# Attention: holding the packed reciprocal and the division's product behind later additions in VectorE's queue

## The chip, the cores and the metric

The program runs on one core of a Trainium2 chip. The metric is the device time of one execution in microseconds (us). Before the change it is 2966.07 us, the median of three runs (2962.72 to 2966.71). The profiled execution of the same kernel spans 2957.4 us; the times inside the stage below are read from it.

## The reference

The whole program is a convolution-attention block, a multi-head attention and a mixture of experts, one after the other. Only the attention is touched: 4096 tokens, 256 channels, 8 heads of 32 channels each.

```python
q, k, v = jnp.split(x @ w_qkv + b_qkv, 3, axis=-1)        # then split into heads
dots = jnp.einsum('bhid,bhjd->bhij', q, k) * d ** (-0.5)
attn = jax.nn.softmax(dots, axis=-1)
out = jnp.einsum('bhij,bhjd->bhid', attn, v)
...
return out @ w_out + b_out
```

The softmax is computed as exp(dots), summed over the keys, and the product with v is divided by that sum afterwards.

## The kernel before

**Loops.** The attention (L958 to L1057) runs over 8 chunks of 512 queries (`qc`), and in each over two groups of four heads (`g`). That makes 16 groups, which are numbered 0 to 15 here in the order in which they run, so that an even number has g = 0 and an odd one g = 1. Each group runs over 32 tiles of 128 keys (`i` from 0 to 31).

**One tile of keys.** TensorE multiplies keys with queries for the four heads (L968) into two PSUM tiles of two banks each (`ps_two`, three of which exist, so a tile takes two out of three). ScalarE takes the exponential of each pair of heads (L978) into one SBUF tile `pe` of 128 x 2048 numbers; four such tiles exist (`bufs=4`), so tile i needs the buffer of tile i - 4. A `pe` has two readers: TensorE multiplies it with the values, one tile later, into `acc` (L938, called by `use`), and VectorE adds it to `total`, the running sum over the keys, in two additions of 128 x 1024 (L985). Tile 0 is not added by itself: the first addition is of tiles 0 and 1. Tile 31 isn't added either, but goes straight to the denominator by a multiplication with ones. So a group has 60 additions. `total` is a single buffer.

**The end of a group.** It is spread over the first tiles of the next group. `behind` hands a list of stages to `tick`, and every tile calls `tick` once, after its additions are written. At tile 0 `take` does the last product and copies `acc` to `attnT` (ScalarE, L1003). At tile 1 `pack` multiplies `total` with ones on TensorE (the denominators, L1006), copies them to SBUF (ScalarE, L1024), and sends one row of each head to DRAM and back in another layout, as 128 x 16 numbers (`dens`, `some`, L1026 and L1027, from the SP queue). Since the first addition of a group overwrites `total`, it waits for the multiplication of tile 1. Some tiles later `turn` takes the reciprocal of the 128 x 16 numbers on VectorE (L1032), stores it to DRAM (L1033) and reads it back, spread over each head's 32 partitions (L1036, four transfers). Later still `spread` multiplies the 128 x 512 numbers of `attnT` by it on VectorE (L1009). The last group divides at once, without this round trip.

**Projections.** In every group with g = 1 except that of the first chunk (groups 3, 5, ... 15), four tiles (i = 3, 10, 17, 24) also project the previous chunk: two products on TensorE (L919), an addition and two statistics instructions on VectorE (L922, L740, L741).

**What sets the order on an engine.** The text of the program isn't the order of an engine's queue: the framework's scheduler orders the instructions of each engine, subject to the dependencies that it knows. In the text, `turn` stands behind the additions of tile 6, and `spread` behind those of tile 11. In the queue of VectorE the scheduler has both earlier:

```
L985 total<-pe        x2     tile 1
L985 total<-total,pe  x2     tile 2
L1032 reciprocal             `turn`
L985 total<-total,pe  x3     tile 3, and half of tile 4
L1009 act<-act,rec           `spread`
L985 total<-total,pe  x53    the rest
```

Of the kernel before, what the change touches and what calls it, by code (L numbers as in the profile page):

```python
# [111 lines left out]
def tile_conv_attn_hybrid(ctx: ExitStack, tc: tile.TileContext, a: dict, out: bass.AP):  # L112
    nc = tc.nc
# [4 lines left out]
    def psum(name, bufs):  # L118
        return tc.tile_pool(name=name, bufs=bufs, space=PSUM)
# [20 lines left out]
    def tok(i):  # L140
        return slice(P * i, P * (i + 1))

    def chunk(i):
        return slice(CH * i, CH * (i + 1))
# [18 lines left out]
    def behind(*stages):  # L163

        chains.append(list(stages))

    def tick():
        due = chains[:]
        chains.clear()
        for stages in due[::-1]:  # L170
            stages[0]()
        chains.extend(stages[1:] for stages in due if stages[1:])

    def flush():
        while chains:
            tick()
# [584 lines left out]
    with ExitStack() as phase:  # L761
# [163 lines left out]
        with tc.If(tame > 0) as branch:  # L925
            with (
                tc.tile_pool(name="a_work", bufs=1) as work,
                tc.tile_pool(name="a_dram", bufs=1, space=bass.MemoryType.DRAM) as dram,
                psum("a_ps1", 1) as ps,
            ):  # L930

                def two_banks():
                    return ps.tile([P, 2, CH], F32, tag="two", name="ps_two", bufs=3)

                def per_head(to, lhsT, rhs, start, stop):

                    for hd in range(4):
                        nc.tensor.matmul(  # L938
                            to[D * hd : D * (hd + 1), :],
                            lhsT(hd),  # L940
                            rhs[:, hd, :],
                            start=start,
                            stop=stop,
                            skip_group_check=True,
                        )

                dens = dram.tile([4, CH], F32, name="dens")  # L950
                recs = dram.tile([4, CH], F32, name="recs")
                packed = lambda z: z.rearrange("h (j c) -> (h j) c", c=CH // D)
                done = []

                def den_bank():
                    return ps.tile([P, CH], F32, tag="den", name="ps_den")

                for qc in range(NCH):  # L958
                    for g in range(KC):
                        acc = ps.tile([P, CH], F32, tag="acc", name="ps_acc")  # L960
                        den = []
                        total = work.tile([P, 4, CH], F32, name="total")
                        first = None
                        for i in range(NT):
                            sc = [two_banks() for _ in range(2)]
                            for hd in range(4):
                                hs = slice(D * hd, D * (hd + 1))
                                nc.tensor.matmul(  # L968
                                    sc[hd // 2][:, hd % 2, :],
                                    qk[hs, 1, g, tok(i)],  # L970
                                    qk[hs, 0, g, chunk(qc)],
                                    start=True,
                                    stop=True,
                                )
                            pe = work.tile([P, 4, CH], F32, name="pe", bufs=4)
                            pairs = [slice(0, 2), slice(2, 4)]
                            for pair, s in zip(pairs, sc):
                                nc.scalar.activation(pe[:, pair, :], s, AF.Exp, scale=C**-0.5)  # L978
                            if i == 0:
                                first = pe  # L980
                            elif i < NT - 1:

                                for pair in pairs:
                                    to = total[:, pair, :]
                                    nc.vector.tensor_add(  # L985
                                        to, first[:, pair, :] if i == 1 else to, pe[:, pair, :]
                                    )
                            tick()

                            def use(i=i, pe=pe, acc=acc, den=den, g=g):  # L990
                                values = lambda hd: v[:, i, P * g + D * hd : P * g + D * (hd + 1)]
                                per_head(acc, values, pe, i == 0, i == NT - 1)
                                if i == NT - 1:
                                    den.append(den_bank())
                                    per_head(den[0], lambda hd: ones, pe, True, False)

                            stages = [use]
                            if i == NT - 1:
                                to = attnT[:, g, chunk(qc)]

                                def take(use=use, to=to, acc=acc):
                                    use()
                                    nc.scalar.copy(to, acc)  # L1003

                                def whole(den=den, total=total):
                                    per_head(den[0], lambda hd: ones, total, False, True)  # L1006

                                def times(rec, to=to):
                                    nc.vector.tensor_mul(to, to, rec)  # L1009

                                def divide(den=den, whole=whole, times=times):
                                    whole()
                                    rec = work.tile([P, CH], F32, tag="rec", name="rec")
                                    nc.vector.reciprocal(rec, den[0])
                                    times(rec)

                                held = []

                                def pack(den=den, whole=whole, held=held):
                                    whole()
                                    rec = work.tile([P, CH], F32, tag="rec", name="rec")
                                    nc.scalar.copy(rec, den[0])  # L1024
                                    some = work.tile([P, CH // D], F32, name="some")
                                    nc.sync.dma_start(dens, rec[::D, :])  # L1026
                                    nc.sync.dma_start(some, packed(dens))  # L1027
                                    held.append(some)

                                def turn(held=held):  # L1030
                                    some = held.pop()
                                    nc.vector.reciprocal(some, some)  # L1032
                                    nc.sync.dma_start(packed(recs), some)  # L1033
                                    rec = work.tile([P, CH], F32, tag="rec", name="rec")
                                    for hd in range(4):
                                        nc.sync.dma_start(  # L1036
                                            rec[D * hd : D * (hd + 1), :], recs[hd].partition_broadcast(D)
                                        )
                                    held.append(rec)

                                def spread(times=times, held=held):
                                    times(held.pop())

                                wait = [lambda: None] * 4
                                if qc == NCH - 1 and g == KC - 1:
                                    stages = [take, divide]
                                else:
                                    stages = [take, pack, *wait, turn, *wait, spread]
                            behind(*stages)


                            if qc and g == KC - 1 and i in (3, 10, 17, 24):
                                done.append(NB * (qc - 1) + len(done) % NB)
                                project(den_bank(), done[-1])
                flush()
                for i in range(len(done), NT):
                    project(two_banks()[:, 0, :], i)  # L1057
# [55 lines left out]
    with ExitStack() as phase:  # L1113
# [49 lines left out]
        with ExitStack() as routing:  # L1163
# [126 lines left out]
            for n in range(2):  # L1290
# [13 lines left out]
                for i8 in range(0, NT, G):  # L1304
                    some = lambda v, n: v[:, i8 : i8 + G].unsqueeze(1).to_broadcast([P, n, G])
# [169 lines left out]
```

## Time and profile before

| what | value |
|---|---|
| time, median of 3 runs | 2966.07 us |
| span of the profile | 2957.4 us |
| TensorE, matmul, busy over the whole span | 2817.9 us (95%) |
| VectorE busy | 2080.4 us (70%) |
| ScalarE busy | 1526.6 us (52%) |
| first exponential to last group's division | about 1157 to 2342 us |
| reciprocal of the round trip, L1032 | 15, of 246 ns each |
| product of the division, L1009 | 16, of 692 ns each |

The attention takes about 40% of the span. The profile gives for every engine its busy time, and for every instruction the idle time of its engine just before it and what ended that idle time (the releaser). The timeline lists instructions in order of time, with runs of equal ones merged; "x53" is 53 instructions in one stretch. TensorE's ends are modelled by the profiler, so its busy time says less than that of the others.

### The profile page before, as it was taken

The numbers are of one execution on the slowest core, as the hardware profiler recorded it, in microseconds if no ns is written. First come the engines' busy times: TensorE is split into PE (matmuls) and PEld (weight loads), VectorE is DVE, ScalarE is ACT, GpSimd is POOL, SyncE is SP. The second block draws the span as 40 slices with busy tenths as digits, with TensorE's granted clock in tenths as the row PEclk, the third lists the DMA queues.
The fourth block names the chain that finished last, engine by engine and source line by source line (L and its number), as shares of the span: only waits on it lengthen the run. The fifth ranks groups of instructions, "written<-read, shape, count | busy, mean of one in ns | idle before, by whom it ended". The sixth has DMA issues, their size and how long they took to land.

```text
span 2957.4 us, 63169 instructions
## 1 busy us (share of the span) xinstructions
PE 2817.9 (95%) x26422; PEld 1366.7 (46%) x26422; DVE 2080.4 (70%) x2975; ACT 1526.6 (52%) x2110; POOL 741.5 (25%) x832
## 2 busy tenths in 40 slices
PE   7899999989999989999999999999999789999996
PEld 5456442736644354222222222222222268888884
DVE  5776767577586877999999999999999821111113
ACT  2242323124233214888888888888888632222222
POOL 4085858109485621000000000000000022222220
PEclk9999999999999989999999999999999879999997
DMA  2000000000000000000000000000000155565565
GB/s 86 6 2 4 2 3 2 7 1 3 4 2 3 1 19 1 5 5 5 5 5 5 5 5 5 5 5 5 5 5 5 35 187 195 191 201 188 189 200 198
DMA packets 92634, 133.29 MB, mean 45 GB/s; under 512 B 16914, under 2 KB 73976, under 8 KB 92340
## 3 DMA queue, kind: packets, MB, share of 16 engines
q1 hardware_dynamic: 78008, 101.12, 10.4%
q0 software_dynamic: 6912, 18.88, 2.2%
q10 hardware_dynamic: 7420, 9.15, 0.9%
q8 instruction: 211, 3.46, 0.5%
q14 instruction: 83, 0.68, 0.1%
HBM read 111.00 MB, written 18.12 MB: 44 GB/s over the span
## 4 chain that ended last, share of the span: by engine, by line
PE 56%; issue 1%; DVE 1%; DMA 1%; ACT 1%; POOL 0%; ACTq 0%; POOLq 0%; DVEq 0%
PE ps_two L968 19%; PE ps_acc L938 16%; PE ps_yp L1396 8%; PE ps_hp L1389 8%; PE ps_den L938 1%; PE ps_den L919 1%; DMA y<-yrows 1%; PE ps_acc L1313 1%; ACT z L1197 1%; PE ps_tp L1364 1%; DVE total L985 1%; DVE t L1433 0%; DMA xs<-zrows,source 0%; ACT pe L978 0%; PE ps_two L919 0%
## 5 line engine op out<-in xcount | busy, mean ns | idle before, releaser
L978 ACT ACTIVATE pe<-ps_two 128x1024 f32<-128x1024 f32 x1024 | 993.1, 1022 | 157.6 <-PE ps_two L968 151.2
L985 DVE TENSOR_TENSOR total<-total,pe 128x1024 f32<-128x1024 f32 x928 | 1057.9, 1213 | 0.0
L968 PE MATMUL ps_two<-qk 32*128 32x512 f32 x4096 | 636.3, 640 | 3.6 <-POOLq L925 1.9
L938 PE MATMUL ps_acc<-pe,v 128*32 128x512 f32 x4096 | 546.4, 605 | 0.1
L533 ACT COPY sm<-ps_sc 128x384 f32<-128x384 f32 (+4 forms) x486 | 232.4, 512 | 463.0 <-PE ps_sc L657 269.4
L537 POOL TENSOR_TENSOR sm<-sm,mask 128x192 f32<-128x192 f32 (+3 forms) x460 | 379.8, 861 | 228.1 <-ACT sm L533 227.6
L968 PEld LDWEIGHTS ps_two<-qk 32*128 32x128 f32 x4096 | 211.9, 183 | 418.7 <-PE ps_two L968 221.3
L537 DVE TENSOR_TENSOR sm<-ps_sc,mask 128x384 f32<-128x384 f32 (+3 forms) x708 | 323.5, 516 | 92.4 <-PE ps_sc L657 91.2
L1390 ACT ACTIVATE hid<-ps_hp,cols 128x256 f32<-128x256 f32 x288 | 136.3, 473 | 382.5 <-PE ps_hp L1389 382.5
L1239 POOL MEMSET on<- 128x256 f32 x1 | 0.3, 311 | 1190.4 <-PE ps_den L938 1190.4
L938 PEld LDWEIGHTS ps_acc<-pe,v 128*32 128x32 f32 x4096 | 80.9, 108 | 389.2 <-issue 376.0
L1389 PE MATMUL ps_hp<-xe,w 128*128 128x256 f32 x1152 | 256.9, 381 | 0.0
L1396 PE MATMUL ps_yp<-w,hid 128*128 128x256 f32 x1152 | 254.6, 379 | 0.0
L657 PE MATMUL ps_sc<-qk 32*128 32x192 f32 (+3 forms) x2688 | 243.8, 444 | 4.6 <-DVE sm L537 2.9
L1396 PEld LDWEIGHTS ps_yp<-w,hid 128*128 128x128 f32 x1152 | 216.5, 190 | 28.0
L1389 PEld LDWEIGHTS ps_hp<-xe,w 128*128 128x128 f32 x1152 | 208.6, 190 | 41.9 <-ACT hid L1390 5.0
L673 PE MATMUL ps_acc<-sm,v 128*32 128x192 f32 (+3 forms) x2688 | 216.6, 423 | 0.8 <-POOL sm L537 0.8
L1368 DVE TENSOR_SCALAR xe<-ps_tp,cols 128x256 f32<-128x256 f32 x72 | 35.8, 539 | 248.7 <-PE ps_tp L1364 228.7
L537 POOL TENSOR_TENSOR sm<-sm,ycut 128x384 f32<-128x384 f32 (+4 forms) x150 | 150.7, 1024 | 145.3 <-ACT sm L533 145.1
L657 PEld LDWEIGHTS ps_sc<-qk 32*128 32x128 f32 x2688 | 125.5, 185 | 123.0 <-DVE sm L537 70.1
L537 DVE TENSOR_TENSOR sm<-ps_sc,ycut 128x512 f32<-128x512 f32 (+4 forms) x250 | 127.5, 561 | 71.2 <-PE ps_sc L588 69.2
L1398 DVE TENSOR_TENSOR y<-ps_yp,b 128x256 f32<-128x256 f32 x72 | 30.5, 424 | 208.0 <-PE ps_yp L1396 208.0
(235 smaller groups left out, 2290.1 us busy)
## 6 DMA issues: line engine op xcount, KB each, us to landing
w<-in_L_ffn_W SPq DMA_DIRECT2D x72, 1024.0 KB
b<-in_L_ffn_b SPq DMA_DIRECT2D x36, 128.0 KB
zrows<-z SPq DMA_DIRECT2D x4, 1024.0 KB
y<-yrows SPq DMA_DIRECT2D x8, 512.0 KB
y<-yrows ACTq DMA_DIRECT2D x8, 512.0 KB
rec<-recs SPq DMA_DIRECT2D x60, 64.0 KB
x<-in_x ACTq DMA_DIRECT2D x4, 512.0 KB
x<-in_x SPq DMA_DIRECT2D x4, 512.0 KB
```

The costliest lines, as they stand in the source:

```text
L533: nc.scalar.copy(sm[:, :used], sc[:, :used])
L537: engine.tensor_mul(to, of, mk.unsqueeze(1).to_broadcast(list(to.shape)))
L657: nc.tensor.matmul(scs[h][:, at : at + n], kT[hs[h], tok(i)], qT[hs[h], CH * ix + CELL * c0 : CH * ix + CELL * c1], start=True, stop=True, ...
L673: nc.tensor.matmul(acc[hs[h], CELL * c0 : CELL * c1], v[:, i, hs[h]], sms[h][:, at : at + n], start=not begun[0], stop=last and at == plac ...
L938: nc.tensor.matmul(to[D * hd : D * (hd + 1), :], lhsT(hd), rhs[:, hd, :], start=start, stop=stop, skip_group_check=True,)
L968: nc.tensor.matmul(sc[hd // 2][:, hd % 2, :], qk[hs, 1, g, tok(i)], qk[hs, 0, g, chunk(qc)], start=True, stop=True,)
L978: nc.scalar.activation(pe[:, pair, :], s, AF.Exp, scale=C**-0.5)
L985: nc.vector.tensor_add(to, first[:, pair, :] if i == 1 else to, pe[:, pair, :])
L1368: nc.vector.tensor_scalar(xe[:, k, :], tp[:, k, :], cols[:, gain], cols[:, shift], op0=ALU.mult, op1=ALU.add,)
L1389: nc.tensor.matmul(hp, w1[:, k, tok(n)], x_now[:, k, :], start=k == 0, stop=k == KC - 1)
L1390: nc.scalar.activation(hid[:, n, :], hp, AF.Gelu, bias=cols[:, n : n + 1])
L1396: nc.tensor.matmul(yp, hid[:, n, tok(j)], w2[:, n, :], start=n == 0, stop=n == NH - 1)
```

## The change

The scheduler may no longer pull the two VectorE instructions ahead. `add` remembers the last addition that was written, and `tc.issue_after(add.ins)` makes an order edge (no semaphore) from it to each instruction that the block writes on the same engine. Each of the two lists of empty stages is one shorter, so `turn` is written behind the additions of tile 5 and `spread` behind those of tile 9.

```diff
+                add = None
...
-                                    nc.vector.tensor_add(
+                                    add = nc.vector.tensor_add(
                                         to, first[:, pair, :] if i == 1 else to, pe[:, pair, :]
                                     )
...
                                 def turn(held=held):
                                     some = held.pop()
-                                    nc.vector.reciprocal(some, some)
+                                    with tc.issue_after(add.ins):
+                                        nc.vector.reciprocal(some, some)
                                     nc.sync.dma_start(packed(recs), some)
...
                                 def spread(times=times, held=held):
-                                    times(held.pop())
-
-                                wait = [lambda: None] * 4
+                                    with tc.issue_after(add.ins):
+                                        times(held.pop())
+                                wait = [lambda: None] * 3
```

The queue of VectorE then has, in a group without projections:

```
L987 total<-pe        x2     tile 1
L987 total<-total,pe  x8     tiles 2 to 5
L1035 reciprocal
L987 total<-total,pe  x8     tiles 6 to 9
L1011 act<-act,rec
L987 total<-total,pe  x42    the rest
```

In a group with projections the first projection's three instructions stand behind the additions of tile 3, so now ahead of the reciprocal, and the second projection's behind those of tile 10, one tile after the product. The orders of TensorE, ScalarE, GpSimd and the SP queue are the same in both programs, as are all instructions and their number. The aim is that the transfers have landed by the time VectorE comes to the instruction that needs them.

## Prediction

> **What bounds the kernel now.** I read the page first, then the table by windows and the waits inside the attention (1157 to 2337 us), then the timelines of VectorE and ScalarE there. The page, engines and costliest groups:
>
> ```profile
> PE 2817.9 (95%) x26422; PEld 1366.7 (46%) x26422; DVE 2080.4 (70%) x2975; ACT 1526.6 (52%) x2110; POOL 741.5 (25%) x832
> ...
> L985 DVE TENSOR_TENSOR total<-total,pe 128x1024 f32<-128x1024 f32 x928 | 1057.9, 1213 | 0.0
> ```
>
> TensorE looks like the bound: in the table by windows it is busy 100% of nearly every stretch of the attention, while VectorE has about 70.8 of 74 us. That is not the whole truth, and ScalarE's timeline shows why. Its lines have start, length, operation, count, and in brackets the idle time before with its releaser; each line is the two exponentials of one tile (group 1):
>
> ```profile
> 1259.43 1.94 ACT L978 ACTIVATE pe<-ps_two 128x1024 f32<-128x1024 f32 x2 [0.21 <-PE ps_two L968]
> 1261.59 1.94 ACT L978 ACTIVATE pe<-ps_two 128x1024 f32<-128x1024 f32 x2 [0.22 <-PE ps_two L968]
> 1263.78 1.94 ACT L978 ACTIVATE pe<-ps_two 128x1024 f32<-128x1024 f32 x2 [0.25 <-PE ps_two L968]
> 1266.05 1.94 ACT L978 ACTIVATE pe<-ps_two 128x1024 f32<-128x1024 f32 x2 [0.33 <-PE ps_two L968]
> 1268.32 1.94 ACT L978 ACTIVATE pe<-ps_two 128x1024 f32<-128x1024 f32 x2 [0.33 <-PE ps_two L968]
> 1270.59 1.94 ACT L978 ACTIVATE pe<-ps_two 128x1024 f32<-128x1024 f32 x2 [0.33 <-PE ps_two L968]
> ```
>
> Up to 1263.78 a tile takes about 2.16 us (1244.35 to 1263.78 is 9 tiles, 2.159 each); from there on exactly 2.27. TensorE is shown 100% busy at both paces, so its own work is not what makes 2.27. The pace of 2.27 is VectorE's: 14 additions take 15.95 us in its timeline, 1.139 us from start to start, and a tile has two, 2.28 us. The pace of 2.16 is the loop of scores and exponential: with three `ps_two` for two a tile, the scores start when the first exponential of the previous tile is done (1247.46 against 1247.48), so about 1.2 + 0.97 us.
>
> So VectorE is slower than the loop by 0.115 us a tile, and falls behind. It may fall behind only as far as the four `pe` buffers reach: ScalarE needs the buffer of four tiles ago, which at the pace of 2.27 means 4 x 2.27 - 1.94 = 7.14 us from the end of a tile's exponentials to the end of its additions (I measure 7.05). At that limit the whole loop runs at VectorE's pace. What brings it there early are its stalls:
>
> ```profile
> 1232.60 2.36 DVE L985 TENSOR_TENSOR total<-pe 128x1024 f32<-128x1024 f32 x2 [2.75 <-ACT pe L978]
> 1237.15 0.24 DVE L1032 RECIPROCAL some<-some 128x16 f32<-128x16 f32 x1
> 1243.70 0.69 DVE L1009 TENSOR_TENSOR act<-act,rec 128x512 f32<-128x512 f32 x1 [2.97 <-DMA rec<-recs]
> 1305.80 2.36 DVE L985 TENSOR_TENSOR total<-pe 128x1024 f32<-128x1024 f32 x2 [1.24 <-PE ps_den L938]
> 1311.26 0.25 DVE L1032 RECIPROCAL some<-some 128x16 f32<-128x16 f32 x1 [0.83 <-DMA some<-dens]
> 1316.50 0.69 DVE L1009 TENSOR_TENSOR act<-act,rec 128x512 f32<-128x512 f32 x1 [1.65 <-DMA rec<-recs]
> 1378.60 2.36 DVE L985 TENSOR_TENSOR total<-pe 128x1024 f32<-128x1024 f32 x2 [1.24 <-PE ps_den L938]
> ```
>
> The product waits for the round trip in all 15 groups. The lines `total<-pe` mark the starts of groups 1, 2 and 3: where VectorE ended the group late, its next first addition is released by the denominator's matmul instead of by ScalarE. Totals, in the waits of the stage (us, times, longest):
>
> ```profile
> DVE act L1009 <- DMA rec<-recs: 21.4, 15, 3.0
> ...
> DVE total L985 <- PE ps_den L938: 12.2, 10, 1.2
> ...
> DVE some L1032 <- DMA some<-dens: 1.4, 2, 0.8
> ```
>
> [...] in the 2.97 us before 1243.70 additions with their `pe` ready stood behind the product, and 53 follow it at once. [...] This path is SP's, with two transfers one behind the other from reciprocal to product; the trace has 4.99 to 6.55 us for the whole, and I use that.
>
> **The change part by part.** *Added and removed instructions:* none; 15 reciprocals of 0.246 us and 15 products of 0.69 us stay, and cost what they did. The order edge has no semaphore. *Moved:* the reciprocal from behind 4 additions to behind 10, the product from 3 additions behind it to 8.
>
> *Do the waits go?* The packed denominators land at most 5.46 us after the first addition of a group (1305.80 to 1311.26, a group that waited). The reciprocal is now reached after 10 x 1.139 = 11.4 us: 5.9 us to spare. From reciprocal to product the trip takes 5.0 to 6.55 us, and 8 additions behind the reciprocal give 0.17 + 8 x 1.139 = 9.3 us: 2.7 us to spare at the worst. So I cost both waits at nothing; additions hide them. Behind the held instructions only additions and projections are queued, and nothing waits for the product soon: the projection that reads it is a whole group away. The SP queue and the single `rec` buffer are free for some 60 us after it.
>
> *What does a group then take?* VectorE's lag behind ScalarE is 1.76 us at tile 2, grows by 28 x 0.113 = 3.2 us to tile 30 (0.113 is group 10: 4.28 at tile 5, 6.66 at tile 26), and by 0.17 for the reciprocal and 0.61 for the product: 5.7 us at the end. That is under the 7.05 at which ScalarE is held, so all tiles run at 2.16. It is also under the lag at which the next group starts late: groups that ended with 5.86 to 6.15 were followed by a start without delay (steps from the first exponential of 3.07 and 2.92 us), those with 6.81 and 7.05 by steps of 2.92 and 3.6 to 3.77, some 0.7 us more.
>
> A free group is thus 29 tiles x 2.158 + 5.97 for the two at its start + 2.21 to the next = 70.76 us. A check: group 10, which hits the limit only in its last two tiles, takes 71.0 from exponential to exponential. A group with four projections has 74.85 (measured groups 3, 9, 11 and 13, from first exponential to first exponential 75.31 to 75.56, less the 0.44 to 0.71 of their late start).
>
> *Sum.* From the first addition of group 1 (1232.60) to that of group 15 (2262.88) it is 1030.28 us now: eight groups without projections (73.20, 72.80, 71.85, 72.64, 71.81, 71.64, 72.97, 71.71, in all 578.6) and six with (74.95, 75.25, 76.03, 74.97, 74.93, 75.53, in all 451.7). Free: 8 x 70.76 + 6 x 74.85 = 1015.2. That is 15.1 us less. The last group ends in the open, its division waiting for the last addition, and so keeps the 0.51 us that its product waits now. In all 15.6 us, about two thirds of the 22.8 us of waits that go, plus boundaries; the rest of the waits was only lag that no one felt.
>
> **The rivals.**
>
> *A, as above:* 2966.07 - 15.6 = 2950.5 us. Its weakest figure is the end lag of 5.7 against the some 6.2 where late starts begin. If all those starts stayed late it gives back 14 x 0.7 = 9.8 at worst; half of that is about 2955.
>
> *B, TensorE is the bound and the stalls are hidden.* For it: busy 100%, and the waits of TensorE's matmuls in the stage, 1.7 us for ScalarE and 0.7 for VectorE, are all that the profile admits. It gives at most 2.4 us, 2963.7, no change that can be told. Against it: the step from 2.16 to 2.27 at the same amount of work, and its place. In group 1 (stall 2.97) it comes at tile 16, in group 2 (2.48) at tile 21, in group 10 (1.40) at tile 30.
>
> *C, slower: the transfer takes longer at the new place and the wait comes back.* The trip would have to exceed 9.3 us. If it doubled from 5.6 (the mean) to 11.2, VectorE would stand 1.9 us a group instead of 22.8 / 15 = 1.52, which is 15 x 0.38 = 5.7 us more: 2971.8. For it: little; the SP queue and the transfers are the same, and no trip in the trace is over 6.55.
>
> **How the numbers follow.** A has 0.83, its partial forms down to 2958 included; B 0.11; C 0.06. The predicted time is A's, 2950.5. The range reaches from 2945, if free tiles run a little faster than those I measured or the run varies as the three before it did (4 us), to 2959, where A with most late starts still in it ends. Faster by over 0.2% (under 2960.1) 0.84, within 0.2% 0.10, slower (over 2972) 0.06.
>
> **What would show it.** In the profile of the changed kernel the wait of the product for `rec<-recs` should be near 0 (21.4 now), that of the reciprocal 0, and that of the first additions for the denominator's matmul 0 or a few tenths (12.2 now). ScalarE's steps should stay near 2.16 to tile 31, with no run of 2.27. Groups should take 70.8 and 74.9 us, and the stage should end some 15 us earlier, all else unmoved. I am wrong if the steps of 2.27 stay, if the starts stay late (then the end lag was over 6.2), or if the wait at the product comes back.

## The result and the profile after

The changed kernel takes 2949.56 us (median of six runs, 2947.92 to 2952.64), against 2963.38 for the kernel before (six runs, 2962.40 to 2966.71). The ratio is 0.9952 with a 95% interval of 0.9939 to 0.9965, so 14 us less (10 to 18). The profiled execution spans 2947.3 us, against 2957.4.

The page, engines, has the same instructions, and VectorE as busy as before:

```profile
PE 2807.9 (95%) x26422; PEld 1359.9 (46%) x26422; DVE 2079.4 (71%) x2975; ACT 1526.5 (52%) x2110; POOL 740.8 (25%) x832
...
L987 DVE TENSOR_TENSOR total<-total,pe 128x1024 f32<-128x1024 f32 x928 | 1058.1, 1215 | 3.3 <-ACT pe L980 3.3
```

VectorE's timeline over group 1 and into group 2:

```profile
1238.88 2.36 DVE L987 TENSOR_TENSOR total<-pe 128x1024 f32<-128x1024 f32 x2 [2.94 <-ACT pe L980]
1241.16 9.16 DVE L987 TENSOR_TENSOR total<-total,pe 128x1024 f32<-128x1024 f32 x8
1250.24 0.24 DVE L1035 RECIPROCAL some<-some 128x16 f32<-128x16 f32 x1
1250.40 9.10 DVE L987 TENSOR_TENSOR total<-total,pe 128x1024 f32<-128x1024 f32 x8
1259.42 0.68 DVE L1011 TENSOR_TENSOR act<-act,rec 128x512 f32<-128x512 f32 x1
1260.02 47.77 DVE L987 TENSOR_TENSOR total<-total,pe 128x1024 f32<-128x1024 f32 x42
1309.60 2.36 DVE L987 TENSOR_TENSOR total<-pe 128x1024 f32<-128x1024 f32 x2 [1.81 <-ACT pe L980]
```

The brackets behind the reciprocal and the product are gone: neither waits. The group takes 70.72 us from first addition to first addition, and the next one doesn't start late: VectorE stands idle for 1.81 us ahead of it, where a late start had 1.24 (the name in this bracket does not tell the two apart, see the part on the prediction). ScalarE's timeline at the end of the same group, tiles 29 to 31 and tile 0 of the next:

```profile
1298.11 1.94 ACT L980 ACTIVATE pe<-ps_two 128x1024 f32<-128x1024 f32 x2 [0.25 <-PE ps_two L970]
1300.23 1.94 ACT L980 ACTIVATE pe<-ps_two 128x1024 f32<-128x1024 f32 x2 [0.18 <-PE ps_two L970]
1302.41 1.94 ACT L980 ACTIVATE pe<-ps_two 128x1024 f32<-128x1024 f32 x2 [0.25 <-PE ps_two L970]
1304.56 1.94 ACT L980 ACTIVATE pe<-ps_two 128x1024 f32<-128x1024 f32 x2 [0.21 <-PE ps_two L970]
```

The step stays 2.16 us to the end, where before it was 2.27 from tile 16 on. VectorE's lag can be read off both fences: its last addition ends at 1260.02 + 47.77 = 1307.79, the exponentials of tile 30 at 1300.23 + 1.94 = 1302.17, which is 5.62 us.

**Where the time went.** I measure the attention from the first addition of group 1 to the reciprocal of the last group's division (L1014, now L1016), since group 0 has no division behind it and is the same work in both kernels. Before, this stretch is 2337.51 - 1232.60 = 1104.91 us, after it 2328.18 - 1238.88 = 1089.30: 15.6 us less. The span fell by only 10.1, because group 1 starts 6.28 us later in this execution (2.6 of it before the first exponential, 3.7 in group 0, see the last section), while what follows the division takes 0.8 less. Neither is from the change, which touches nothing up to there, and other runs have it otherwise. The stretch is read from one profile of each kernel. It is 1089.26 to 1089.31 us in the changed kernel and in the two runs below that have neither a wait nor more work (old places, held far later), while the ratio has an interval of 8 us, so both are given; where transfers are waited for, as in the kernel before, how far the stretch varies was not measured.

### The profile page after: what moved, and what is told of

The parts are those of the page before. It is cut to its first block, busy times and chain, and to the rows that moved or that the text cites. A ratio compares the mean times of both kernels' runs of the same rounds, so it can differ in the third digit from the quotient of the medians.

```text
span 2947.3 us, 63169 instructions
## 1 busy us (share of the span) xinstructions
PE 2807.9 (95%) x26422; PEld 1359.9 (46%) x26422; DVE 2079.4 (71%) x2975; ACT 1526.5 (52%) x2110; POOL 740.8 (25%) x832
## 4 chain that ended last, share of the span: by engine, by line
PE 57%; DVE 1%; DMA 1%; ACT 1%; issue 1%; POOL 0%; SPq 0%; POOLq 0%; ACTq 0%; DVEq 0%
PE ps_two L970 20%; PE ps_acc L938 17%; PE ps_hp L1395 9%; PE ps_yp L1402 8%; PE ps_den L919 1%; PE ps_den L938 1%; DMA y<-yrows 1%; PE ps_tp L1370 1%; PE ps_acc L1319 1%; ACT z L1203 1%; DVE t L1439 0%; DVE total L987 0%; DMA yrows<-y,target 0%; DVE rec L1016 0%; DMA xs<-zrows,source 0%
## 5 line engine op out<-in xcount | busy, mean ns | idle before, releaser
L970 PEld LDWEIGHTS ps_two<-qk 32*128 32x128 f32 x4096 | 205.4, 183 | 420.4 <-PE ps_two L970 225.5
```

Source lines behind the costliest of these rows:

```text
L970: nc.tensor.matmul(sc[hd // 2][:, hd % 2, :], qk[hs, 1, g, tok(i)], qk[hs, 0, g, chunk(qc)], start=True, stop=True,)
```

## The experiments

All edits below are against the changed kernel. Each ratio is to runs of the kernel before that were made alongside; their medians are 2965.55 us for the first four experiments and 2963.72 us for the others, so what can be compared from one experiment to another are the ratios.

The theory T: per group VectorE has a slack of about 0.55 us without projections and 0.65 with them (the lag at which the next group starts late, about 6.15 us, less the end lag). Stalls and work within it are free; what goes beyond it comes back in full as tiles at 2.27 us and as a late start. The rivals: TensorE is the bound and VectorE hidden (R1); VectorE's time counts in full (R2); the place of the two instructions among the additions costs, not the wait (R3).

### The old places without the wait

```diff
 def turn(held=held):
-    with tc.issue_after(add.ins):
-        nc.vector.reciprocal(some, some)
+    with tc.issue_after(add.ins):
+        nc.vector.reciprocal(still[:, 1], still[:, 0])
...
 def spread(times=times, held=held):
-    with tc.issue_after(add.ins):
-        times(held.pop())
+    with tc.issue_after(half.ins):
+        held.pop()
+        times(still[:, 0, :1].to_broadcast([P, CH]))
...
-    stages = [take, pack, *wait, turn, *wait, spread]
+    stages = [take, pack, turn, *wait[:1], spread]
```

`still` is a small tile filled once with 1/4350; `half` is the first addition of a tile.

> The reciprocal and the product stand where they stand before the change (behind the additions of tile 2, and 3 additions later), but read a small resident tile: the reciprocal a constant, the product a constant near the true 1/denominator. The transfers still run, and nothing on VectorE waits for them; the division is by a constant, so this leaves out the true denominator. Theory (the waits use up VectorE's slack of about 0.55 us a group): about 15 us faster than before, like the changed kernel (2949 us), steps of 2.16 us to the end of every group. Rival (the place among the additions costs, not the wait): as before, 2963.

Measured: ratio to the kernel before 0.9947 (0.9933 to 0.9960), median 2948.26 us; the stretch is 1089.3 us, as with the change. VectorE's timeline, group 1:

```profile
1244.09 0.25 DVE L1038 RECIPROCAL still<-still 128x16 f32<-128x16 f32 x1
1244.25 3.42 DVE L989 TENSOR_TENSOR total<-total,pe 128x1024 f32<-128x1024 f32 x3
1247.59 0.68 DVE L1014 TENSOR_TENSOR act<-act,still 128x512 f32<-128x512 f32 x1
1248.19 60.26 DVE L989 TENSOR_TENSOR total<-total,pe 128x1024 f32<-128x1024 f32 x53
```

The order is that of the kernel before, and so are the operations' lengths; only the bracket is missing, and the whole gain is there. R3 falls: the wait is the cost, the place is none.

### Only one of the two held

```diff
 e2_product_not_held:
-    with tc.issue_after(add.ins):
-        times(held.pop())
+    times(held.pop())
 e3_reciprocal_not_held:
-    with tc.issue_after(add.ins):
-        nc.vector.reciprocal(some, some)
+    nc.vector.reciprocal(some, some)
```

> Only the hold of the product is undone: reciprocal behind the additions of tile 5, product 3 additions later, where the scheduler puts it. Theory: a trip of 5.0 to 6.5 us against 0.17 + 3 x 1.14 = 3.6 us leaves a wait of 1.4 to 3 us in every group, in those with projections too (which have 0.5 to 0.7 before), so the whole gain is lost and some 3 us more: 2963 to 2968. Rival (the early reciprocal is what costs, or both halves count alike): 2950 to 2957.

> Only the hold of the reciprocal is undone: reciprocal behind the additions of tile 2, product behind those of tile 9. Theory: no wait is left but some tenths at the reciprocal, which the slack takes in, so the whole gain: 2948 to 2951. Rival (both halves count alike): 2954 to 2958.

Measured without the hold of the product: 1.0013 (1.0006 to 1.0019), about 4 us slower than before, with a stretch of 1112.1 us, 7.2 more than before, where some 3 were expected. Its waits in the attention (us, times, longest):

```profile
DVE act L1011 <- DMA rec<-recs: 30.1, 15, 3.1
DVE total L987 <- PE ps_den L938: 17.2, 14, 1.2
```

The product waits 30.1 us instead of 21.4. In the groups with projections, three VectorE instructions of a projection used to lie between reciprocal and product and covered a part of the trip; now they lie ahead of the reciprocal, and these groups wait 1.5 us and more, too (before 0.5 to 0.7, once 1.85). All 14 starts are late. So holding the reciprocal alone, which only moves the wait, isn't neutral but a loss.

Measured without the hold of the reciprocal: 0.9949 (0.9935 to 0.9963), a stretch of 1089.6 us. The reciprocal waits in two groups, 1.3 us together, the product never. The hold of the product, with more additions ahead of it, brings the whole gain here; that of the reciprocal brings at most 0.3 us of the stretch.

### Half the cover

```diff
-    stages = [take, pack, *wait, turn, *wait, spread]
+    stages = [take, pack, *wait, turn, *wait[:1], spread]
```

> As changed, but the product only 4 additions behind the reciprocal, not 8: 0.17 + 4 x 1.14 = 4.7 us of cover for a trip of 5.0 to 6.5 us. Theory: a wait of 0.3 to 1.8 us a group, some 0.9 in the mean, of which 0.55 is free: about 6 us slower than the changed kernel, 2953 to 2958. Rival (any wait counts in full): 13 us slower, 2963; rival (TensorE is the bound): 2949.

Measured: 0.9966 (0.9952 to 0.9979); the stretch is 1095.8 us, 6.5 more than with the change. The waits:

```profile
DVE act L1011 <- DMA rec<-recs: 13.0, 15, 1.9
```

13.0 us of waits cost 6.5. By T group by group it should be 6.1: of the 14 groups ahead of the last, seven have waits below the slack (0.35 to 0.52 us) and cost nothing, three lie about at it (0.62 to 0.74) and cost 0.1 each, four have 1.18 to 1.92 and cost their excess, and the last group's 1.85 counts in full. R1 (0) and R2 (13) both fall.

### More work for VectorE, without any wait

```diff
     with tc.issue_after(add.ins):
-        times(held.pop())
+        rec = held.pop()
+        times(rec)
+        for _ in range(n):       # n = 1 and n = 3
+            nc.vector.tensor_mul(rec, rec, rec)
```

> As changed, with one more product of 128x512 on VectorE behind the division's in each of 15 groups (it squares the spent reciprocals), 0.61 us of queue each. Theory (a slack of 0.5 to 0.65 us a group): nearly free, 0 to 1.5 us slower than the changed kernel, 2949.5 to 2951. Rival (VectorE's time counts in full): 15 x 0.61 = 9.2 us slower, 2959. Rival (TensorE is the bound and VectorE hidden): 0.

> The same with three: 1.83 us of queue a group. Theory: 1.83 less the slack is 1.2 to 1.3 us a group, 18 to 20 us slower than the changed kernel, 2967 to 2970, with late starts and steps of 2.27 us at the end of groups. Rival (in full): 27.5 us, 2977. Rival (TensorE is the bound): 0.

Measured with one: 0.9956 (0.9943 to 0.9970), the stretch 1091.5 us, 2.2 more than with the change. With three: 1.0034 (1.0021 to 1.0048), which is 24 us more than with the changed kernel, and a stretch of 1110.6, 21.3 more; VectorE's lag ends at 7.05 us in groups 1 to 15, and the pace of 2.27 is back at their ends. VectorE's timeline with three, group 1:

```profile
1258.10 0.68 DVE L1011 TENSOR_TENSOR act<-act,rec 128x512 f32<-128x512 f32 x1
1258.82 1.42 DVE L1049 TENSOR_TENSOR rec<-rec 128x512 f32<-128x512 f32 x2
1260.15 1.22 DVE L987 TENSOR_TENSOR total<-total,pe 128x1024 f32<-128x1024 f32 x1
1261.29 0.68 DVE L1049 TENSOR_TENSOR rec<-rec 128x512 f32<-128x512 f32 x1
1261.89 46.63 DVE L987 TENSOR_TENSOR total<-total,pe 128x1024 f32<-128x1024 f32 x41
1309.76 2.36 DVE L987 TENSOR_TENSOR total<-pe 128x1024 f32<-128x1024 f32 x2 [1.24 <-PE ps_den L938]
```

I had priced an extra product at 0.61 us, which is what the division's takes of the queue ahead of an addition (1259.42 to 1260.02 in the changed kernel). But the first squaring overwrites what the product ahead of it still reads, and starts 0.72 us after the product's start, when that has ended (1258.10 to 1258.82); the third, which the scheduler put behind an addition, takes 0.60 again. From first to last addition a group's VectorE work is 68.91 us with the change, 69.63 with one extra, 70.96 with three, so 0.72 and 2.05 us. With this price and the slacks of 0.55 and 0.65 T gives, for three extra, 8 x 1.50 + 6 x 1.40 in the groups and 2.05 in the open at the end, 22.5 us; measured are 21.3 (1.48 in a group without projections, 1.0 to 1.3 in one with them). R2 with the same price is 15 x 2.05 = 31. The expectation of 18 to 20 was missed by the price. One extra costs 1.5 us over 14 groups, where R2 has 10, and 0.7 at the end, where nothing hides it; that end had been left out of the expected 0 to 1.5 us. R1 falls with both.

T is a rule of thumb and not exact. Worked out from the waits group by group, the loss against the changed kernel is 14.7 us for the kernel before (measured 15.6), 21.8 without the hold of the product (22.8), 6.1 with half the cover (6.5), 2.5 and 22.5 with one and three extra products (2.2 and 21.3).

### Three buffers instead of four

```diff
-pe = work.tile([P, 4, CH], F32, name="pe", bufs=4)
+pe = work.tile([P, 4, CH], F32, name="pe", bufs=3)
```

> As changed, with three pe buffers instead of four. Theory: the lag at which ScalarE is held falls from 7.1 to 3 x 2.27 - 1.94 = 4.9 us, below the end lag of 5.4 to 5.6, so the last tiles run at 2.27: 0.55 to 0.75 us a group, 9 to 11 us slower than the changed kernel, 2958 to 2961. Rival (the ring of buffers isn't what couples VectorE to TensorE): no change, 2949.5.

Measured: 0.9986 (0.9979 to 0.9994), the stretch 1100.7 us, 11.4 more than with the change. ScalarE's timeline at the end of group 1:

```profile
1284.52 1.94 ACT L980 ACTIVATE pe<-ps_two 128x1024 f32<-128x1024 f32 x2 [0.30 <-PE ps_two L970]
1286.61 1.94 ACT L980 ACTIVATE pe<-ps_two 128x1024 f32<-128x1024 f32 x2 [0.15 <-PE ps_two L970]
1288.87 1.94 ACT L980 ACTIVATE pe<-ps_two 128x1024 f32<-128x1024 f32 x2 [0.31 <-PE ps_two L970]
1291.14 1.95 ACT L980 ACTIVATE pe<-ps_two 128x1024 f32<-128x1024 f32 x2 [0.33 <-PE ps_two L970]
1293.41 1.94 ACT L980 ACTIVATE pe<-ps_two 128x1024 f32<-128x1024 f32 x2 [0.33 <-PE ps_two L970]
```

These are tiles 22 to 26. The pace of 2.27 us is back, though VectorE waits for no transfer and has no gap inside a group. With four buffers and the same order no tile of groups 1 to 15 is held at it. The lag stops at 4.78 us in groups 1 to 15 (expected 4.9), and a group takes 0.5 to 0.95 us more. So it is the ring of `pe` buffers through which VectorE slows ScalarE and, behind it, TensorE. The brackets name TensorE all the same. What holds ScalarE is seen where an exponential is set beside the addition that frees its buffer, here tile 26 of group 1 in the kernel before, whose buffer is that of tile 22:

```profile
1285.18 1.21 DVE L985 TENSOR_TENSOR total<-total,pe 128x1024 f32<-128x1024 f32 x1
1286.49 1.02 ACT L978 ACTIVATE pe<-ps_two 128x1024 f32<-128x1024 f32 x1 [0.33 <-PE ps_two L968]
```

The exponential starts 0.1 us after the addition has ended, and so it is from tile 16 to tile 31 of that group, and with three buffers from tile 23 on (0.09 to 0.11 us each). In the changed kernel the addition has ended 1.4 us or more ahead of every exponential of groups 1 to 15. `pe` has a second reader, TensorE's product with the values, but in the held tiles looked at (20 to 30 of group 1 in the kernel before) the last such product ahead of the exponential ended 1.36 us before it.

### Held far later

```diff
-    stages = [take, pack, *wait, turn, *wait, spread]
+    stages = [take, pack, *wait, *wait, *wait, turn, *wait, *wait, *wait, spread]
```

> As changed, but held far later: reciprocal behind the additions of tile 11, product behind those of tile 21. Theory: nothing waits for the product, and what counts is only that the transfers are hidden, as they are already: no change, 2948 to 2951. Rival (there is still a cost of the place, or someone waits for the product): a few us either way.

Measured: 0.9956 (0.9942 to 0.9969), the stretch 1089.3 us: no change. Once the transfers are hidden, the place is free over at least twelve tiles, and nobody waits for the product.

## Why the prediction was right

**The waits go.** Right: the product's 21.4 us and the reciprocal's 1.4 are 0, and the run with the old places shows that it was they that cost. The cover of 9.3 us is 9.18 in the profile (1250.24 to 1259.42), and with 4.7 the wait was back.

**A free group.** Right: 70.76 and 74.85 us were worked out, and 70.69 to 70.76 and 74.81 to 75.17 are measured from first addition to first addition. Groups 1 to 14 together were put at 1015.2 us and take 1015.27.

**The end lag.** Right: 5.7 was worked out, and 5.5 to 5.6 is measured in groups without projections, 5.2 to 5.5 in those with them; no start is late. The margin, which was rival A's weakest figure, is as thin as I thought: one extra product of 0.7 us uses it up.

**The last group in the open.** 0.51 us was put down for it; from its first addition to its division it takes 74.03 us instead of 74.63, which is 0.60 less.

**The sum.** 15.6 us predicted, 15.6 in the stretch. The measured difference of the medians, 13.8 us, is less by 2, within its interval. That the predicted 2950.5 comes so near to 2949.56 is in part luck: over six runs the kernel before has a median of 2963.4, not the 2966.1 that I started from.

**A sign that I named wrongly.** I expected the wait of the first additions for the denominator's matmul near 0; the waits have 7.5 us in 4 groups. That is no late start. The prediction read from the label that a late group is started by this matmul and one in time by ScalarE, but in all groups from 1 on, in both kernels, the first addition starts 0.10 to 0.20 us after the end of this matmul. The label goes to the matmul in four groups of the changed kernel because the second exponential of tile 1 ends 0.02 us after the addition's start there, and to ScalarE in the other eleven because it ends 0.06 us before it. What tells a late start is the length: in groups that VectorE starts late it idles 1.21 to 1.24 us, the way from its own last addition through the matmul to the next first one, and now it idles 1.8 to 2.9 us ahead of every group. The shorter idle time was the costly one.

**The rivals.** TensorE as the bound (B) is refuted by the three-buffer run and by three extra products, in which TensorE's work is the same. The wait that comes back (C) did so only where I took the cover away.

## What to carry to other kernels

While the product waited for its transfer, 2.97 us in group 1 of the kernel before, nothing behind it in VectorE's queue ran, and 53 additions followed it at once. So look at the queue and not at the text: here the scheduler had moved the product ahead. What such a wait cost was read from the lag of VectorE against ScalarE: up to the first limit that the lag met, less the lag that VectorE's own work builds up, it was free, and beyond that it came back about one for one (of 13.0 us of waits with half the cover, 6.5, where the excess over the slack is 6.1). Here the first limit was the end of the group, at a lag of about 6.15 us, and the second the ring of four buffers, at 7.05; what lies beyond showed as late starts (VectorE idle for 1.21 to 1.24 us ahead of a group, where the changed kernel has 1.78 to 2.94) and as a slower pace (2.27 us a tile instead of 2.16) of a TensorE that the profile shows as 100% busy at both. A bracket names the signal that came last by the profile, which need not be what held the engine (in the held tiles of group 1 of the kernel before it names TensorE, where the addition that frees the buffer ended 0.1 us ahead); start times beside end times tell more. Hold the last instruction of the round trip far enough behind the one that starts it (here eight additions, 9.18 us, for trips of at most 6.55 in the kernel before); moving the first alone moved the wait along (30.1 us instead of 21.4).

## What I had not expected of the hardware

The first microseconds of the attention ran at half clock in the profiled execution of the changed kernel. The table by windows (window, length, busy us of TensorE, its weight loads, VectorE, ScalarE and GpSimd with instruction counts, then the granted clock, DMA share, GB/s):

```profile
1158.00:1162.00 4.00, 2.50 (x12) 0.78 (x12) 0.08 (x1) 2.14 (x2) 0.00 (x0) 0.73 0.00 2
1162.00:1166.00 4.00, 3.78 (x12) 0.70 (x12) 1.80 (x2) 3.02 (x4) 0.00 (x0) 0.50 0.00 0
1166.00:1170.00 4.00, 4.00 (x24) 0.74 (x20) 1.35 (x2) 1.76 (x2) 0.00 (x0) 0.50 0.00 0
1170.00:1174.00 4.00, 4.00 (x36) 1.15 (x32) 3.39 (x4) 2.85 (x4) 0.00 (x0) 0.99 0.00 2
```

By this table the granted clock is 0.50 for 10.2 us, and TensorE gets through 24 matmuls in a window where the next has 36. Group 0 took 74.7 us, from its first addition to that of group 1, instead of 71.0 in the kernel before, where the granted clock is 1.00 in each of these four windows. `e1_places_no_wait` has 1.00 in every window from 1140 to 1200 and a group 0 of 71.2 us. In `e3_reciprocal_not_held` group 0 took 74.7 us, too, with the gaps of the changed kernel between VectorE's first additions (2.65 and 0.59 us against 2.65 and 0.61). Group 0 has the same instructions in the same order in the kernel before and the changed one, so the change is not its cause. Why the clock was lower in one execution and not in another was not shown, and no run was made to move it.
